# Seven block products in place of eight for a feed-forward product, accumulated and read in PSUM

## The chip, the cores and the metric

The kernel runs on one core of a Trainium2 chip. The metric is the device time of one launch in microseconds, as the median of several runs: 3187.57 us for the kernel before (3 runs, 3185.76 to 3188.36). The profile is of one execution with a span of 3186.1 us from the first to the last instruction.

## The reference

64 graphs of 256 nodes with 256 features each go through two layers. All data are f32, the adjacency is int32.

```
# layer 0
h = gat(x, adj, W1, a1); h = gat(h, adj, W2, a2)          # graph attention
h = layernorm(x + h)
ff = relu(h @ w_ff1 + b_ff1) @ w_ff2 + b_ff2              # (256 -> 1024 -> 256)
x = layernorm(h + ff)
# layer 1
q, k = x @ Wq + bq, x @ Wk + bk                           # 8 heads of 32
attn = softmax(q @ k.T / sqrt(32))
out = sum over r of (attn * (adj == r)) @ (x @ Wv[r] + bv[r])
x = layernorm(x + out @ Wo + bo)
ff = gelu(x @ W1 + b1) @ W2 + b2                          # (256 -> 1024 -> 256)
return layernorm(x + ff)
```

The product that is changed is `h @ w_ff1` of layer 0. Transposed, and for two graphs together, it is a matrix of 1024 x 256 weights by one of 256 x 512 activations.

## The kernel before, in words

The 64 graphs are worked on as 32 pairs. Each pair goes one way (`whole_way`): graph layers (`gat_layers`), feed-forward of layer 0, attention, feed-forward of layer 1, and a store. A matmul takes a stationary operand of 128 x 128 and a moving one of up to 512 columns, and writes into one of eight PSUM banks of 128 x 512 f32 (`bank`).

The order of the work is written by a planner in the kernel's own Python (`run`). Each pair's way is a generator. At each `yield` it names the events that the next step of TensorE needs, a stage that only one pair may be in ("gat", "ff", "attention"), and the number of banks that it takes. Work for the other engines is handed over with `put(engine, us, emit, *events, rank, ...)`: a piece with an estimated duration, which is emitted when its events have happened by the planner's clock; a lower rank goes first. `took(us)` moves TensorE's clock on. Up to three pairs are under way at a time. A TensorE step counts as sure when its inputs were ready `SLACK` microseconds ago by the planner's clock; among the sure ones those that are not in the stage "ff" go first; if none is sure, the one that is ready earliest is taken. What comes out is one fixed order of instructions for each engine; the waits between engines are added by the framework by what each instruction reads and writes.

Both feed-forwards are in `feed_forward`. For each of eight blocks `m` of 128 hidden features two products of 512 columns are accumulated over the two halves of the 256 input features (L538), and ScalarE adds the bias and applies relu or gelu on the way to SBUF (L541). The second product (L553) takes those eight tiles as stationary operands, 32 products of 256 columns. VectorE adds the result to the rows (L442 in `add_rows`), `layernorm` follows on VectorE (L454 to L464) with a power on GpSimd (L467), and `transposed` turns the rows by way of VectorE (L484) and DMAs to and from HBM on the queue of SyncE (`home`, `yT`).

The transposed activations `yT` lie so that a view `p k (b a) i` gives 512 columns of one input half `c`; k is one of two column halves of 256 columns, in runs of 32.

Other parts that the change touches: `load` brings in `xT`, the int32 adjacency `adjT` (three buffers) and `x` on SyncE's queue. `gat_layers` looks for nodes without neighbours in `adjT` (L387, L388), `gat_weights` uses it in L367, and `attention` multiplies the exponentials by it (L617). `attention` has tiles `qT`, `kT`, `oT`; scores read qT (L606), `products` write oT (L648), `into_rows` multiplies oT by Wo (L657). `relieve` (L732) takes a correction out of the biases at the start.

Of the kernel before, what the change touches and what calls it, by code (L numbers as in the profile page):

```python
# [27 lines left out]
SLACK = 1.5  # L28
# [4 lines left out]
def two_layers(ctx: ExitStack, tc: tile.TileContext, t: dict, out: bass.AP, flag: bass.AP):  # L33
# [91 lines left out]
    def bank():  # L125
# [13 lines left out]
                                             ("xT", 1), ("rows", 1), ("e", 2), ("adjT", 3), ("x", 4))}  # L139
# [137 lines left out]
    def load(pair, at=None):  # L277
# [7 lines left out]
        def adjT():  # L285
            to["adjT"] = io.tile([P, 4, N], I32, name="adjT", bufs=3)
            nc.sync.dma_start(to["adjT"], t["adjT"][rows].rearrange("b (c p) n -> p (b c) n", p=P))
# [7 lines left out]
        for emit in (xT, adjT, x):  # L295
            takes(emit.__name__, free[emit.__name__] != [])
            emit()
# [57 lines left out]
    def gat_weights(y, at, at_home, ratio, there, to, empty, b):  # L355
# [3 lines left out]
        def weigh(j):  # L359
# [7 lines left out]
            nc.vector.scalar_tensor_tensor(e[:, j], to["adjT"][:, k], empty[:, k:k + 1], e[:, j],  # L367
# [13 lines left out]
    def gat_layers(pair, to, loads):  # L381
# [3 lines left out]

        def largest():
# [7 lines left out]
        emptied = put("vector", 1.35, largest, loads[1], rank=2)  # L394
# [44 lines left out]
    def add_rows(y, p, b, *events):  # L439

        rows = y[:, of_graph(b), :].rearrange("p k d -> p (k d)")
        return put("vector", 0.6, lambda: nc.vector.tensor_tensor(rows, p, rows, ALU.add), *events, frees=["bank"])  # L442

    def layernorm(r, gb, b, *events):
# [4 lines left out]
        def statistics():  # L449
# [6 lines left out]
            nc.vector.tensor_scalar(rstd, mv[:, :, 1], EPS, None, ALU.add)  # L456
# [9 lines left out]
        there = put("vector", 1.15, statistics, *events)  # L466
        power = put("gpsimd", 0.8, lambda: nc.gpsimd.tensor_tensor(rstd, rstd, mhalf[:, :2], ALU.pow), there)  # L467
        return put("vector", 0.8, scale, power, put("vector", 0.8, centre, there))
# [55 lines left out]
    def feed_forward(y, normal, w, func, relieved, gb, pair, stage):  # L524
        w1, b1, w2 = w
        onwards = stage == 0
        if hurried(pair, stage):
            yield from transposed_on_tensor(y, normal)
        f, evacuated = [], []
        for m in range(NF):  # L530
            if m == 0:
                yield [normal[0], normal[1]], "ff", 1
                yT = [normal["yT"].rearrange("p b a (c k i) -> p c k (b a) i", c=KC, k=2)[:, c] for c in range(KC)]
            else:
                yield [], None, 1
            p1 = bank()
            for c in range(KC):
                nc.tensor.matmul(p1, lhsT=w1[:, c, m * P:(m + 1) * P], rhs=yT[c],  # L538
                                 start=c == 0, stop=c == KC - 1)
            f.append(work.tile([P, 512], F32, name="ff", bufs=NF))  # L540
            there = put("scalar", 0.6, lambda m=m, p1=p1: nc.scalar.activation(f[m], p1, func, bias=b1[:, m:m + 1]),  # L541
                        took(1.72), relieved, function="gelu" if func == AF.Gelu else None, frees=["bank"])
            evacuated.append(there)
        frees_at(clock["tensor"], ["yT"])
        for b in range(2):
            for j in range(2):
                k, split = 2 * b + j, NF // 2 if b or j else NF - 2
                for part in (range(split), range(split, NF)):
                    yield evacuated[part[0]:part[-1] + 1] if k == 0 else [], None, j == 0 and part[0] == 0
                    if j == 0 and part[0] == 0:  # L550
                        p2 = bank()
                    for m in part:
                        nc.tensor.matmul(p2[:, j * D:(j + 1) * D], lhsT=f[m][:, (2 * j + b) * P:(2 * j + b + 1) * P],  # L553
                                         rhs=w2[:, m, :], start=m == 0, stop=m == NF - 1)
                    there = took(0.43 * len(part))
# [3 lines left out]
        done_with("ff")  # L559

# [649 lines left out]
```

## Time and profile before

| what | value |
|---|---|
| median of the timed runs | 3187.57 us |
| span of the profiled execution | 3186.1 us |
| granted TensorE clock | 0.996 |
| HBM traffic | 137.51 MB read, 64.73 MB written |
| DMA engines' mean rate | 64 GB/s |

In the profile, PE is TensorE's matmuls, PEld its weight loads, DVE is VectorE, ACT is ScalarE, POOL is GpSimd, SP is SyncE; a "q" after it is the engine's sequencer. L538 is line 538 of the kernel. A group of instructions is written as: line, engine, operation, written tile <- read tiles, elements written <- read, count | busy us, mean ns of one | idle us of the engine just before them, and what ended that idle time. The chain of waits is the work that ended last, followed back from the end to the start. In a window of time the columns after its length are the busy us of PE, PEld, DVE, ACT and POOL with counts of instructions, then the granted clock, the share of the DMA engines and GB/s.

An f32 matmul is written as two instructions in the profile, so 16 products appear as x32.

### The profile page before, as it was taken

The page shows a single profiled execution, that of the slowest core. Times are in us where ns is not written, and L with a number is a line of the kernel's source. Part 1 is how long each engine was busy: PE and PEld are TensorE (multiplying, and loading weights), DVE is VectorE, ACT ScalarE, POOL GpSimd, SP SyncE. Part 2 cuts the span into 40 slices and gives each one's busy share as a digit, 9 for nine tenths or more (in the row PEclk, how much of TensorE's full clock was granted, in tenths as well). Part 3 has the DMA queues.
Part 4 walks back from the last instruction along what each step waited for, and adds up shares of the span by engine and source line. Part 5 has one row for each costly group of instructions (what it writes and reads, how often), then busy time and mean ns, then how long its engine had stood idle before and what let it go on. Part 6 is the DMA issues. An engine that isn't in the chain of part 4 may idle for free.

```text
span 3186.1 us, 45043 instructions
## 1 busy us (share of the span) xinstructions
PE 3150.4 (99%) x16830; PEld 2019.1 (63%) x16830; DVE 2210.0 (69%) x5525; ACT 1142.7 (36%) x2074; POOL 200.9 (6%) x262
## 2 busy tenths in 40 slices
PE   7999999999999999999999999999999999999998
PEld 6656756675576567566655765675666557656655
DVE  4677667767776776677677757766776777577564
ACT  3334333432432333334324323333342244333332
POOL 0000000000000000000000000000000000000000
PEclk8999999999999999999999999999999999999999
DMA  5112311321131123113211311231122113112200
GB/s 180 41 41 74 93 47 47 93 80 40 54 100 60 34 74 97 47 44 93 83 37 54 100 60 34 74 99 49 39 93 85 35 54 103 57 37 64 66 1 15
DMA packets 209857, 205.27 MB, mean 64 GB/s; under 512 B 22112, under 2 KB 169696, under 8 KB 209632
## 3 DMA queue, kind: packets, MB, share of 16 engines
q1 hardware_dynamic: 209632, 202.32, 20.4%
q8 instruction: 135, 2.21, 0.3%
q14 instruction: 90, 0.74, 0.1%
HBM read 137.51 MB, written 64.73 MB: 63 GB/s over the span
## 4 chain that ended last, share of the span: by engine, by line
PE 98%; DVE 1%; DMA 0%; ACT 0%; SPq 0%; issue 0%; POOL 0%; POOLq 0%; DVEq 0%
PE ps L538 28%; PE ps L553 28%; PE ps L574 7%; PE ps L566 7%; PE ps L635 7%; PE ps L606 4%; PE ps L416 4%; PE ps L429 4%; PE ps L657 3%; PE ps L400 3%; PE ps L638 2%; PE ps L732 0%; PE ps L515 0%; DMA w_L_gnn_w_ff1p<-in_L_gnn_w_ff1p 0%; DVE s L647 0%; DMA right<-in_L_gnn_W 0%
## 5 line engine op out<-in xcount | busy, mean ns | idle before, releaser
L617 DVE TENSOR_TENSOR m<-a,adjT 128x512 f32<-128x512 f32 x512 | 350.6, 685 | 208.1 <-ACT a L613 208.1
L553 PE MATMUL ps<-w_L_gnn_w_ff,ff 128*128 128x256 f32 x2048 | 463.3, 380 | 0.0
L553 PE MATMUL ps<-w_L_gnn_W,ff 128*128 128x256 f32 x2048 | 458.3, 380 | 0.0
L538 PE MATMUL ps<-yT,w_L_gnn_W1p 128*128 128x512 f32 x1024 | 456.9, 598 | 0.7 <-ACT yT L519 0.7
L538 PE MATMUL ps<-yT,w_L_gnn_w_ff1p 128*128 128x512 f32 x1024 | 452.2, 594 | 1.1 <-ACT yT L519 1.1
L553 PEld LDWEIGHTS ps<-w_L_gnn_w_ff,ff 128*128 128x128 f32 x2048 | 387.2, 190 | 90.9 <-issue 43.0
L553 PEld LDWEIGHTS ps<-w_L_gnn_W,ff 128*128 128x128 f32 x2048 | 388.2, 190 | 82.0 <-issue 30.4
L613 ACT ACTIVATE a<-ps 128x512 f32<-128x512 f32 x512 | 264.4, 602 | 392.7 <-issue 212.6
L467 POOL TENSOR_TENSOR rstd<-rstd,mhalf 128x2 f32<-128x2 f32 x256 | 200.2, 782 | 2978.8 <-DVE rstd L456 2978.8
L538 PEld LDWEIGHTS ps<-yT,w_L_gnn_W1p 128*128 128x128 f32 x1024 | 192.7, 191 | 224.9 <-issue 204.6
L538 PEld LDWEIGHTS ps<-yT,w_L_gnn_w_ff1p 128*128 128x128 f32 x1024 | 192.7, 190 | 224.7 <-issue 208.0
L647 DVE RECIPROCAL s<-ps 128x256 f32<-128x256 f32 x128 | 224.9, 1757 | 129.8 <-PE ps L638 129.8
L442 DVE TENSOR_TENSOR x<-ps,x 128x512 f32<-128x512 f32 x256 | 174.4, 681 | 200.8 <-PE ps L553 178.4
L541 ACT ACTIVATE ff<-ps,c_L_gnn_b_ff 128x512 f32<-128x512 f32 x256 | 175.8, 688 | 348.3 <-PE ps L538 348.3
L566 PE MATMUL ps<-wv,yTa 128*128 128x512 f32 x512 | 238.7, 599 | 0.0
L365 DVE SCALAR_TENSOR_TENSOR e<-rows,ratio 128x256 f32<-128x256 f32 x256 | 122.0, 477 | 149.7 <-DMA rows<-row 137.8
L375 ACT ACTIVATE xw<-xw,rs 128x258 f32<-128x258 f32 (+1 forms) x256 | 115.2, 501 | 288.3 <-DVE rs L370 288.3
L541 ACT ACTIVATE ff<-ps,c_L_gnn_b 128x512 f32<-128x512 f32 x256 | 169.1, 686 | 133.8 <-PE ps L538 133.1
L621 DVE TENSOR_TENSOR h<-a 128x256 f32<-128x256 f32 x512 | 213.5, 417 | 0.0
L454 DVE BATCH_NORM_STATS2 st<-x 128x6 f32<-128x256 f32 x512 | 208.2, 407 | 4.1
L391 ACT ACTIVATE xw<-ps 128x260 f32<-128x260 f32 (+1 forms) x256 | 97.7, 389 | 220.9 <-PE ps L416 111.4
L566 PEld LDWEIGHTS ps<-wv,yTa 128*128 128x128 f32 x512 | 94.6, 190 | 120.3 <-issue 117.9
(99 smaller groups left out, 3529.2 us busy)
## 6 DMA issues: line engine op xcount, KB each, us to landing
home<-yb SPq DMA_DIRECT2D x182, 256.0 KB, 2.0
yT<-home SPq DMA_DIRECT2D x728, 64.0 KB, 2.0
rows<-row SPq DMA_DIRECT2D x60, 512.0 KB, 4.1
xT<-in_xT SPq DMA_DIRECT2D x32, 512.0 KB, 3.6
adjT<-in_adjT SPq DMA_DIRECT2D x32, 512.0 KB, 4.0
x<-in_x SPq DMA_DIRECT2D x32, 512.0 KB, 4.0
out<-x SPq DMA_DIRECT2D x32, 512.0 KB, 3.4
w_L_gnn_w_ff1p<-in_L_gnn_w_ff1p SPq DMA_DIRECT2D x1, 1024.0 KB, 7.5
```

What stands on the lines that cost most here:

```text
L454: nc.vector.bn_stats(st[:, j, :], rows[j])
L467: power = put("gpsimd", 0.8, lambda: nc.gpsimd.tensor_tensor(rstd, rstd, mhalf[:, :2], ALU.pow), there)
L538: nc.tensor.matmul(p1, lhsT=w1[:, c, m * P:(m + 1) * P], rhs=yT[c], start=c == 0, stop=c == KC - 1)
L541: there = put("scalar", 0.6, lambda m=m, p1=p1: nc.scalar.activation(f[m], p1, func, bias=b1[:, m:m + 1]), took(1.72), relieved, function= ...
L553: nc.tensor.matmul(p2[:, j * D:(j + 1) * D], lhsT=f[m][:, (2 * j + b) * P:(2 * j + b + 1) * P], rhs=w2[:, m, :], start=m == 0, stop=m == N ...
L566: nc.tensor.matmul(ps, lhsT=yT[:, b, c, jc * P:(jc + 1) * P], rhs=wv[:, c].rearrange("p r m -> p (r m)"), start=c == 0, stop=c == KC - 1)
L574: nc.tensor.matmul(ps, lhsT=w[:, d, c * P:(c + 1) * P], rhs=yT[:, :, d, :], start=d == 0, stop=d == KC - 1)
L613: nc.scalar.activation(a[n][o], ps[o], AF.Exp)
L617: nc.vector.tensor_tensor(m[n][o], a[n][o], adj, ALU.mult)
L621: nc.vector.tensor_tensor(h[n][o], a[n][o][:, :N], a[n][o][:, N:], ALU.add)
L635: nc.tensor.matmul(po[o * DH:(o + 1) * DH, :N], lhsT=v[b][:, jc, at:at + DH], rhs=e[o][:, jc * N:(jc + 1) * N], start=r == jc == 0, stop=r ...
L647: there = put("vector", 1.68, lambda: nc.vector.reciprocal(s, po[:, N:]), there, rank=0)
```

## The change

The 1024 x 256 by 256 x 512 product is cut into 2 x 2 blocks on each side: A's four blocks of 512 x 128, B's four of 128 x 256. It is computed with seven products of blocks in place of eight, by a scheme in which the sums of blocks are made ahead and the partial results are shared between output blocks. The sums of weights are made once at the start (`block_sums`), the three more sums of activations for each pair on VectorE (`first_sum`, `other_sums`). For each of four block rows `t` of 128:

- `begin`: product 0 into half x of a bank, product 1 into half w of another, product 2 into half z of the first. ScalarE copies x out (u1), and VectorE adds w to it, which gives the first output block.
- `sixth`: product 3 on top of what stands in x; ScalarE copies the sum out (u2).
- `seventh`: product 4 on top of that; copied out (u3), and VectorE adds z to it, the fourth output block.
- `fourth`: product 6 on top of that; ScalarE takes relu of x, the third output block.
- `third`: product 5 on top of z; VectorE adds z to u2, the second output block.

Relu of the other blocks is taken from SBUF. The steps of four block rows are staggered, and the second feed-forward product is started in pieces among them. Layer 1's feed-forward keeps the old form (`whole`).

Besides: SLACK is 0.5 in place of 1.5, and some estimated durations differ. The adjacency is copied to bytes by ScalarE (`small_adj`, three buffers), and the int32 one keeps one buffer (pair 1 borrows a tile of `v`). oT takes qT's place. The addition of epsilon in the layernorm moves from VectorE to GpSimd. The first layer's weights come in four transfers. The buffers of the last check (`kept`) are borrowed from others.

```diff
-SLACK = 1.5
+SLACK = 0.5
...
-            nc.vector.tensor_scalar(rstd, mv[:, :, 1], EPS, None, ALU.add)
+        def root():
+            nc.gpsimd.tensor_scalar(rstd, mv[:, :, 1], EPS, None, ALU.add)
+            nc.gpsimd.tensor_tensor(rstd, rstd, mhalf[:, :2], ALU.pow)
...
+        def small_adj():
+            to["adj"] = io.tile([P, 4, N], U8, name="adj", bufs=3)
+            nc.scalar.activation(to["adj"], to["adjT"], AF.Copy)
...
+        def product(to, n, t, rhs, first=False):
+            nc.tensor.matmul(to, lhsT=w1[:, n, t * P:(t + 1) * P], rhs=rhs, start=first, stop=True, skip_group_check=True)
+            return took(0.43)
...
+        def begin(t):
+            q = of[t]
+            yield [normal[0], normal[1], summed[0], relieved] if t == 0 else [], "ff" if t == 0 else None, 2 if t % 2 == 0 else 1
...
+            xz = bank()
+            q["x"], q["z"] = xz[:, :N], xz[:, N:]
+            q["w"] = of[t - 1]["w"] if t % 2 else bank()
+            q["u1"] = evacuate(f[t][:, :N], q["x"], product(q["x"], 0, t, B[0][0], True))
+            there = product(q["w"][:, t % 2 * N:t % 2 * N + N], 1, t, B[1][0], t % 2 == 0)
+            q["c11"] = accumulate(f[t][:, :N], q["w"][:, t % 2 * N:t % 2 * N + N], q["u1"], there, frees=["bank"] * (t % 2))
+            product(q["z"], 2, t, sums[:, 0])
+
+        def sixth(t):
+            q = of[t]
+            yield [q["u1"], summed[1]], None, 0
+            q["u2"] = evacuate(f[t][:, N:], q["x"], product(q["x"], 3, t, sums[:, 1]))
+
+        def seventh(t):
+            q = of[t]
+            yield [q["u2"], summed[2]], None, 0
+            q["u3"] = evacuate(f[t + half][:, N:], q["x"], product(q["x"], 4, t, B[0][1]))
+            q["c22"] = accumulate(f[t + half][:, N:], q["z"], q["u3"])
+
+        def fourth(t):
+            q = of[t]
+            yield [q["u3"], summed[3]], None, 0
+            q["c21"] = activate(f[t + half][:, :N], q["x"], t + half, 0.36, product(q["x"], 6, t, sums[:, 2]))
+
+        def third(t):
+            q = of[t]
+            yield [q["c22"]], None, 0
+            c12 = accumulate(f[t][:, N:], q["z"], q["u2"], product(q["z"], 5, t, B[1][1]))
+            put("vector", 0.0, lambda: None, c12, q["c21"], rank=-1, lag=0.0, frees=["bank"])
+            evacuated[t + half] = activate(f[t + half][:, N:], f[t + half][:, N:], t + half, 0.36, q["c22"], q["c21"])
+            evacuated[t] = activate(f[t], f[t], t, 0.6, q["c11"], c12)
...
+        def first_by_blocks():
+            for t in range(half):
+                yield from begin(t)
+                if t > 1:
+                    yield from fourth(t - 2)
+                    yield from third(t - 2)
+                if t:
+                    yield from seventh(t - 1)
+                yield from sixth(t)
+            for step in (lambda: second(0, 0, (0, half), 1), lambda: second(0, 1, (0, half)),
+                         lambda: fourth(half - 2), lambda: third(half - 2), lambda: seventh(half - 1),
+                         lambda: second(0, 0, (1, half + 1)), lambda: second(0, 1, (1, half + 1)),
+                         lambda: fourth(half - 1), lambda: third(half - 1)):
+                yield from step()
...
-        qT, kT, oT = (work.tile([P, KC, 512], F32, name=n) for n in ("qT", "kT", "oT"))
+        qT, kT = (work.tile([P, KC, 512], F32, name=n) for n in ("qT", "kT"))
+        oT = qT
...
+    def block_sums(w, there):
+        for to, a, b, op in ((4, 0, 2, ALU.subtract), (2, 2, 6, ALU.add), (3, 2, 0, ALU.subtract), (5, 1, 3, ALU.subtract)):
+            there = put("vector", 0.65, lambda to=to, a=a, b=b, op=op: nc.vector.tensor_tensor(w[:, to], w[:, a], w[:, b], op),
+                        there, rank=0)
+        return there
```

## The prediction

> **What bounds the kernel now.** I read the busy shares first, then the chain of waits, then the groups of instructions, then the busy time in chosen windows.
>
> ```profile
> PE 3150.4 (99%) x16830; PEld 2019.1 (63%) x16830; DVE 2210.0 (69%) x5525; ACT 1142.7 (36%) x2074; POOL 200.9 (6%) x262
> PE 98%; DVE 1%; DMA 0%; ACT 0%; SPq 0%; issue 0%; POOL 0%; POOLq 0%; DVEq 0%
> ```
>
> The second line is the chain: 98% of the span is TensorE itself, so nothing but TensorE sets the time, apart from start and tail (in the first 70 us PE is busy 51.9, in the last 87 us 71.8). So TensorE time taken out is gained, if no new wait replaces it. The price of a product is best read in the chain in order of time (start, duration, instructions), because durations of single matmuls are modelled while runs of them are not:
>
> ```profile
> 674.12 12.09 PE ps L553 x56
> ...
> 691.38 13.73 PE ps L538 x32
> ```
>
> Each f32 product counts as two instructions. 13.73 us are the 16 products of 512 columns of one first feed-forward product: 0.858 each. 12.09 us are 28 products of 256 columns: 0.432 each. The groups:
>
> ```profile
> L553 PE MATMUL ps<-w_L_gnn_w_ff,ff 128*128 128x256 f32 x2048 | 463.3, 380 | 0.0
> L538 PE MATMUL ps<-yT,w_L_gnn_w_ff1p 128*128 128x512 f32 x1024 | 452.2, 594 | 1.1 <-ACT yT L519 1.1
> L541 ACT ACTIVATE ff<-ps,c_L_gnn_b_ff 128x512 f32<-128x512 f32 x256 | 175.8, 688 | 348.3 <-PE ps L538 348.3
> L391 ACT ACTIVATE xw<-ps 128x260 f32<-128x260 f32 (+1 forms) x256 | 97.7, 389 | 220.9 <-PE ps L416 111.4 <-PE ps L400 109.4
> L648 DVE TENSOR_TENSOR oT<-ps,s 128x256 f32<-128x256 f32 x128 | 53.8, 420 | 2.2
> L621 DVE TENSOR_TENSOR h<-a 128x256 f32<-128x256 f32 x512 | 213.5, 417 | 0.0
> L456 DVE TENSOR_SCALAR rstd<-mv 128x2 f32<-128x2 f32 x256 | 43.2, 169 | 8.9
> ```
>
> L538 has waited 1.1 us in the whole run: every one of its products was ready to go. The other lines are prices for what the change adds. Last, windows (duration, then busy us of PE, PEld, DVE, ACT, POOL):
>
> ```profile
> 1822.14:1834.16 12.02, 12.02 (x30) 5.32 (x29) 11.26 (x35) 5.61 (x10) 1.48 (x2) 1.00 0.50 153
> 1856.62:1870.35 13.73, 13.73 (x33) 6.08 (x32) 9.48 (x26) 5.34 (x8) 1.52 (x3) 1.00 0.36 111
> 1565.27:1856.62 291.35, 291.35 (x1538) 186.32 (x1536) 207.21 (x517) 106.14 (x192) 18.75 (x25) 1.00 0.21 66
> ```
>
> The third is one period of three pairs: 97.1 us a pair, PE never idle. The first two are this product of two of the three pairs. It runs there nearly alone on PE, and DVE is already 94% and 69% busy with layernorms and graph weights of other pairs. The third pair's (1605 to 1630) lies in pieces between attention steps.
>
> **What the Trainium skill says.** "PSUM — Partial Sum Buffer", section "The four PSUM rules": a first matmul clears the accumulate bits of the whole bank, later ones overwrite where the bit is clear and add where it is set, and a synchronised read in the midst of a group is allowed; so the seven-product scheme can work as written. The same page, "PSUM bank collisions raise a hardware error": two engines must not touch one bank in the same quadrant at once, even in different columns. No run here shows it; in the kernel before, PE fills a bank and one engine then empties it. "TensorE: Matmul & The Clock Gate", "Back-to-back issue gap": time goes with columns plus about 2.5 ns a matmul; the trace agrees (215.9 ns against half of 429.1, so 1.4 ns per instruction). "ScalarE: Activation LUTs", "What ACT_TABLE_LOAD costs": 186 ns plus 0.833 ns per column, 93 more for a bias pointer, that is 403 for 260 columns; the trace has 389.
>
> **The change part by part.**
>
> PE, per pair: 16 x 0.858 = 13.73 goes, 28 x 0.432 = 12.09 comes (the line shown). Saved 1.64, over 32 pairs 52.5 us. Twelve more weight loads of 0.190 lie under matmul instructions of 0.216, as they do at L553. The second product is only cut differently.
>
> ACT, per pair: 8 x 0.688 goes; 12 copies, 4 relus from PSUM and 4 from SBUF of 256 columns at 0.389 and 4 relus of 512 at 0.688 come: 10.5 - 5.5 = 5.0. The adjacency's copy to bytes has 1024 columns: by 0.389 for 260 and 0.688 for 512, some 1.0 to 1.3. In all +6 a pair, 194 us: 42% busy.
>
> DVE, per pair: 12 accumulations at 0.420 and 4 block sums at 0.417 come, 6.7; eight L456 go, 1.35. Net 5.4, 171 us: 75% busy. On average both have room. The byte adjacency I cost at nothing for L617 and L367: the int32 operand at L367 takes 485 ns, the f32 one at L365 477. It can hardly be slower than 5% of 685.
>
> POOL gets the epsilon add ahead of each power, about one more 0.78 us operation; L464 waited for POOL only 23.4 us in all. DVE time is not the end here: nothing, at most 2 us in the tail.
>
> SP: the weights come in four transfers in place of one (three more issues of about 0.43 us, same bytes); needed at 21 us for the bias, and the first product starts at 68. The block sums of the weights (4 x 0.68) also end long before that. The int32 adjacency has one buffer: a load placed early would hold SP, and the yT gathers queued behind it. It is freed by L387, early in a pair, so nothing; up to 5 us if not. oT in qT's place makes the next pair's L575 wait for L657, which ended at 1640.72 just as the next Wq product (1.72 us) began; that activation can't come before its end. Nothing.
>
> **Waits that come in.** Now the same PSUM half is filled, read by ACT, and filled on top, four times per block row; PE depends on ACT and DVE inside the product. The round trip: ACT starts 0.20 after the last instruction's slot ends (the product from 1822.14 gives its four slots at 1823.86, L541 starts at 1824.06), the copy takes 0.39, and PE goes on 0.05 after an ACT end (yT done at 3147.35, L538 at 3147.40): 0.64. `begin` issues three products in one step, first into x, third into z of the same bank. The first copy is emitted after them, so, with banks kept apart, it starts only when the third is through: 0.86 later than the planner thinks. Then for block row 0 `sixth` follows at once: PE stands 0.64. For row 1 one product lies between: 0.64 - 0.43 = 0.21. From row 2 three lie between (1.30): none. At the end the second product of rows 3 and 7 has four products (1.73) ahead of it, against relu of half a tile, accumulate, relu of 512: 0.20 + 0.39 + 0.42 + 0.20 + 0.69 + 0.05 = 1.95, and one more slip between ACT and DVE in that bank: about 0.3. Sum 1.15 a pair if nothing is put between. Below, such a wait can be zero (other pairs' steps fill it, or the bank isn't shared in practice); above, see the third rival. I take it as met in two of three pairs, since one of three lies among attention steps: 0.77 x 32 = 24.5 us.
>
> SLACK 0.5 lets the planner pick a step whose inputs were ready 0.5 us ago where it wanted 1.5. PE has nothing to win from that in the steady part, and loses if ACT or DVE run late; I take it with the waits.
>
> **Sum.** 3186.1 - 52.5 + 24.5 + 1 (tail) = 3159.1 against this execution's span; the timed runs' median lies 1.5 us above it (3187.57), so 3161.
>
> **Rivals.** A change of under 0.2%, 6.4 us, can't be told from none.
>
> 1. All of it is gained: the waits find other work. For: ACT is at 36%, and the steps are staggered by four products or more. Against: two of three such products run alone. 3187.6 - 52.5 = 3135.
> 2. The gain is eaten to the last: waits of 1.6 a pair. About 3187, within 0.2%.
> 3. The other side: DVE paces the product. 6.7 us of its work come into windows where it already has 9.5 to 11.3 of 12 to 13.7. Its pieces are not interrupted (statistics and its kin are about 1.2 us: 1822.01 to 1823.20), so an accumulation stands up to 1.2 us in line, and PE's `fourth` and `third` stand behind it, as both use that bank. From copy to end of the accumulation 0.64 + 0.20 + 0.42 = 1.26 must fit in the four products (1.73) before `fourth`: 0.47 is left. The gain is gone when this costs (1.64 - 0.77) / 4 = 0.22 per block row; at 0.4 per row it is 1.6 + 0.77 - 1.64 = 0.73 a pair, +23 us: 3211. Against it: the planner gives accumulations first rank and knows the lengths.
>
> **How the numbers follow.** Forecast 0.48, full gain 0.18, nothing 0.10, slower 0.24. Faster is 0.48 + 0.18 = 0.66. For the range: the full gain with a little more from start or tail is 3133; the third rival's price is 3212. Both signs lie inside; the forecast's own range is 3140 (a quarter of the waits) to 3180 (waits of 1.4 a pair).
>
> **What would show it.** PE busy some 52 us less, with 256-column products at 216 ns a slot. Idle time of PE before the product's lines, put down to ACT, about 25 us; put down to DVE and over 30 us, the third rival. ACT near 42%, DVE near 75%. A gap ahead of the fourth product of a block row in a lone window, 0.6 us, would show the shared bank; its lack, the first rival. Wrong altogether if the attention or graph lines begin to wait: then it is the planner's order, not the product.

## The result, and the profile after

The changed kernel takes 3196.16 us (median of 6 runs, 3193.16 to 3197.79) against 3186.95 us for the kernel before (6 runs): a ratio of 1.0028, 95% interval 1.0015 to 1.0041. By the bound of the prediction, 0.2%, it is slower, though the interval's lower end lies inside that bound. The forecast of 3161 is 35 us too low. The profiled executions differ by 9.5 us (3195.6 against 3186.1), as the medians do, so the two traces can be set beside each other.

From the page of the changed kernel, the busy shares, and the chain of waits by engine:

```profile
PE 3131.6 (98%) x17598; PEld 2151.9 (67%) x17598; DVE 2336.6 (73%) x5785; ACT 1309.7 (41%) x2612; POOL 267.5 (8%) x518
PE 86%; DVE 4%; DMA 4%; ACT 3%; issue 1%; SPq 1%; POOL 0%; ACTq 0%; DVEq 0%; POOLq 0%
```

PE is busy 18.8 us less than before (3150.4), and the span is longer all the same. The chain says what kind of time came in: it was 98% PE, and is 86% now, with VectorE, ScalarE and, new, DMA.

The groups of the changed product, its copy and its accumulation (line, engine, operation, tiles and count | busy us, mean ns | idle before, releaser):

```profile
L571 PE MATMUL ps<-yT,w_L_gnn_w_ff1p 128*128 128x256 f32 x1024 | 269.6, 380 | 0.0
L571 PE MATMUL ps<-sums_yT,w_L_gnn_w_ff1p 128*128 128x256 f32 x768 | 231.4, 393 | 18.8 <-ACT ff L575 15.3 <-DVE ff L578 0.2
L575 ACT ACTIVATE ff<-ps 128x256 f32<-128x256 f32 x384 | 142.8, 382 | 235.2 <-PE ps L571 231.2
L578 DVE TENSOR_TENSOR ff<-ps,ff 128x256 f32<-128x256 f32 x384 | 160.7, 419 | 135.1 <-ACT ff L581 55.3 <-ACT ff L575 54.2 <-PE ps L571 24.2
```

The products that wait are those with block sums as moving operand: `sixth` and `fourth` are among them. (Busy time of matmuls overlaps, so these 501 us are no measure of the product.) The waits of TensorE and of its weight loads (engine, line, what was waited for: us, times, longest):

```profile
PEld ps L571 <- ACT ff L575: 37.2, 52, 0.9
PEld ps L571 <- DVE ff L578: 23.3, 61, 0.7
PEld ps L424 <- ACT xw L379: 19.3, 16, 3.0
PE ps L571 <- ACT ff L575: 15.3, 31, 0.5
PE ps L424 <- ACT xw L379: 13.2, 10, 2.6
```

Two places: the changed product (L571), and a product of the graph layers (L424, L416 before), which the change doesn't touch and whose weight loads before waited 0.7 us for the same. A weight load's wait and its matmul's wait overlap, and the first begins early, so neither column is the time lost. For that I took, from the trace, the starts of TensorE's matmul instructions. The time from one start to the next is a slot. The median slot of a line is its normal price, and what lies above it is a loss: a gap where it is 0.11 us or more, a restart where it is about 0.10 (see the last section). Us over the whole span:

| | before | after | difference |
|---|---|---|---|
| normal slots of layer 0's first product | 439.3 | 387.1 | -52.2 |
| normal slots of all else | 2666.6 | 2661.8 | -4.8 |
| gaps ahead of L571 | 0 | 31.7 | +31.7 |
| gaps ahead of layer 0's second product, L627 | 0 | 5.0 | +5.0 |
| gaps ahead of L424 | 0 | 13.8 | +13.8 |
| other gaps (first 70 us: 16.2 and 16.6) | 21.6 | 22.9 | +1.3 |
| restarts, 425 and 561 | 42.1 | 56.2 | +14.1 |
| small deviations | -0.4 | -0.2 | +0.2 |
| first to last start | 3169.1 | 3178.3 | +9.2 |

(439.3 is half of what L538 had in both layers. The products on parts of the array, the attention's and the one that turns rows at the start and the end, L515 before and L526 after, are counted with all that passes in their slots. Of the 4.8 us in the second line 3.7 come from L515, which waits at the end of the kernel before.) So the gain is there to within a microsecond, and 66 us of losses came against it: about 51 in and around the product, about 14 in the graph layers.

Shortly before its end the changed kernel is further behind than these 9.2 us. The last matmul of the last pair's graph layers starts at 2987.2 us before and at 3004.5 after, 17.3 us later. What follows up to the last start takes 190.0 us before and 181.5 after. About 3 of these 8.5 us can be the new product's saving; for the rest see SLACK below.

The timeline of the changed kernel where a product starts (start, us, what; in brackets idle time before and its releaser), and the window over it (length, then busy us of PE, PEld, DVE, ACT, POOL, clock, DMA share, GB/s):

```profile
1574.25 1.03 PE L571 MATMUL ps<-yT,w_L_gnn_w_ff1p 128*128 128x256 f32 x4
1575.11 0.59 PE L571 MATMUL ps<-sums_yT,w_L_gnn_w_ff1p 128*128 128x256 f32 x2
1575.74 0.38 ACT L575 ACTIVATE ff<-ps 128x256 f32<-128x256 f32 x1 [3.98 <-PE ps L571]
1576.18 0.70 PE L571 MATMUL ps<-sums_yT,w_L_gnn_w_ff1p 128*128 128x256 f32 x2 [0.47 <-ACT ff L575]
```
```profile
1574.25:1587.07 12.82, 12.30 (x56) 10.01 (x54) 9.90 (x30) 7.10 (x18) 2.77 (x6) 1.00 0.13 41
```

The first line is the products into x and w of `begin`, the second the one into z. They come at 0.432 a product: x is done at about 1574.68. Its copy starts at 1575.74, which is 0.20 after z is done. `sixth` starts at 1576.18, where the slot after z would have ended at 1575.54: 0.64 us of standing, and its second instruction comes 0.10 late. In the window DVE is busy 77% and ACT 55%; neither is full.

### The profile page after: what moved, and what is told of

The parts are those of the page before. It is cut to its first block, busy times and chain, and to the rows that moved or that the text cites. A ratio compares the mean times of both kernels' runs of the same rounds, so it can differ in the third digit from the quotient of the medians.

```text
span 3195.6 us, 47479 instructions
## 1 busy us (share of the span) xinstructions
PE 3131.6 (98%) x17598; PEld 2151.9 (67%) x17598; DVE 2336.6 (73%) x5785; ACT 1309.7 (41%) x2612; POOL 267.5 (8%) x518
## 4 chain that ended last, share of the span: by engine, by line
PE 86%; DVE 4%; DMA 4%; ACT 3%; issue 1%; SPq 1%; POOL 0%; ACTq 0%; DVEq 0%; POOLq 0%
PE ps L627 24%; PE ps L571 11%; PE ps L636 10%; PE ps L688 7%; PE ps L680 7%; PE ps L750 7%; PE ps L721 4%; PE ps L424 4%; PE ps L437 4%; PE ps L772 4%; PE ps L408 3%; DMA rows<-row 2%; PE ps L753 2%; ACT ff L581 1%; DVE m L732 1%
## 5 line engine op out<-in xcount | busy, mean ns | idle before, releaser
L627 PE MATMUL ps<-w_L_gnn_w_ff,ff 128*128 128x256 f32 x2048 | 473.1, 382 | 1.3
L627 PE MATMUL ps<-w_L_gnn_W,ff 128*128 128x256 f32 x2048 | 459.6, 381 | 0.0
L732 DVE TENSOR_TENSOR m<-a,adj 128x512 f32<-128x512 f32 x512 | 351.2, 686 | 127.7 <-ACT a L728 127.7
L627 PEld LDWEIGHTS ps<-w_L_gnn_W,ff 128*128 128x128 f32 x2048 | 386.5, 190 | 75.7 <-issue 26.1
L627 PEld LDWEIGHTS ps<-w_L_gnn_w_ff,ff 128*128 128x128 f32 x2048 | 384.4, 190 | 72.1 <-ACT ff L581 10.5
L466 POOL TENSOR_SCALAR rstd<-mv 128x2 f32<-128x2 f32 x256 | 71.8, 280 | 2899.9 <-DVE mv L463 2701.6
L571 PE MATMUL ps<-yT,w_L_gnn_w_ff1p 128*128 128x256 f32 x1024 | 269.6, 380 | 0.0
L578 DVE TENSOR_TENSOR ff<-ps,ff 128x256 f32<-128x256 f32 x384 | 160.7, 419 | 135.1 <-ACT ff L581 55.3
L571 PE MATMUL ps<-sums_yT,w_L_gnn_w_ff1p 128*128 128x256 f32 x768 | 231.4, 393 | 18.8 <-ACT ff L575 15.3
L575 ACT ACTIVATE ff<-ps 128x256 f32<-128x256 f32 x384 | 142.8, 382 | 235.2 <-PE ps L571 231.2
L571 PEld LDWEIGHTS ps<-yT,w_L_gnn_w_ff1p 128*128 128x128 f32 x1024 | 193.6, 190 | 33.0 <-issue 4.2
```

Source lines behind the costliest of these rows:

```text
L571: nc.tensor.matmul(to, lhsT=w1[:, n, t * P:(t + 1) * P], rhs=rhs, start=first, stop=True, skip_group_check=True)
L732: nc.vector.tensor_tensor(m[n][o], a[n][o], adj, ALU.mult)
```

## The experiments

The theory: (a) the shared bank makes the copy late, as the prediction had it, and (b) the losses ahead of L424 come from another edit. The rivals: VectorE has too much to do; or the order of the steps is to blame, above all SLACK. Ratios are to the kernel before in runs on the same chip, with the 95% interval. "Gaps" and "restarts" are those of the table above, each from one trace.

### All but the product

`rest` has every other edit, and the old eight products (and with them the first layer's weights in one transfer again).

```diff
-        half, by_blocks = NF // 2, stage == 0
+        half, by_blocks = NF // 2, False
```

> Layer 0's first product in the old form (16 products of 512 columns), all other edits of the change kept: SLACK 0.5, byte adjacency, epsilon on GpSimd, oT in qT's place, estimated durations. If the seven products alone bring the waits: as before, within 5 us (3187). If SLACK 0.5 or the other edits cost something by themselves, as the 12.6 us of waits ahead of L424 in the changed kernel suggest: slower than before by 10 to 20 us (3197 to 3207), with gaps ahead of the graph layer's products.

3189.34 us, 1.0008 (1.0001 to 1.0015). So the product by itself, on top of the other edits, costs 3196.2 - 3189.3 = 7 us where it should save. And the other edits have a loss of their own: gaps of 14.8 us ahead of L424, as large as in the changed kernel. They don't come from the seven products. Neither branch of what was expected is met whole: the time is nearly that of the first, the gaps are those of the second.

### x in a bank of its own

```diff
-            xz = bank()
-            q["x"], q["z"] = xz[:, :N], xz[:, N:]
-            q["w"] = of[t - 1]["w"] if t % 2 else bank()
+            wz = bank()
+            q["x"], q["w"], q["z"] = bank()[:, :N], wz[:, :N], wz[:, N:]
...
```

Every `begin` takes two banks, eight for the four rows in place of six, and they are given free one by one.

> The changed kernel with x alone in a bank, and w and z of one block row together in another (8 banks for four rows in place of 6). Theory bank: the first copy waited for the third product only because both are of one bank, so the wait ahead of sixth falls from 0.64 to under 0.1 for row 0 (20 us over 32 pairs, with the restarts 24) and from 0.14 to none for row 1 (4 to 6 us), and fourth no longer waits for VectorE's reading of z (9 to 14 us): some 30 to 40 us faster than the changed kernel, about 3160. Theory round trip: TensorE to ScalarE to TensorE is too slow at any placing, or ScalarE is busy: the gaps stay, 3190 to 3200. Two more banks may bring waits for banks: then new gaps at begin.

3166.49 us, 0.9940 (0.9926 to 0.9953): 30 us less than the changed kernel. The start of the product, in its timeline:

```profile
1554.27 1.03 PE L571 MATMUL ps<-yT,w_L_gnn_w_ff1p 128*128 128x256 f32 x4
1554.90 0.38 ACT L575 ACTIVATE ff<-ps 128x256 f32<-128x256 f32 x1 [2.32 <-PE ps L571]
1555.13 1.03 PE L571 MATMUL ps<-sums_yT,w_L_gnn_w_ff1p 128*128 128x256 f32 x4
```

The copy now starts 0.63 us after the product began, where it was 1.49: 0.86 earlier, two products, to the digit. It ends at 1555.28, and `sixth`, which is in the last line's four instructions, follows z without a break. What L571's instructions waited for (idle us, times), in the changed kernel:

```profile
  ACT ff L575: 52.4, 83
  DVE ff L578: 23.6, 62
```

and with x alone:

```profile
  ACT ff L575: 2.6, 6
  DVE ff L578: 2.1, 3
```

Both are gone, VectorE's too, with the same number of VectorE instructions. Gaps ahead of L571 fall from 31.7 to 2.1 and all restarts from 56.2 to 39.8. That is 46 us; the runs gained 30. What took the difference can be seen: the slots of the attention's products on parts of the array grew by 19 us, the scores from 138.0 to 150.6 (L719) and the products with v from 222.5 to 227.0 (L748), with the output sums 2 more. The growth is in single pairs: the scores of five of the 32 have slots of 6.6 to 7.0 us in place of 4.3. In one of these stretches they stand in line behind VectorE:

```profile
1081.44 1.21 PE L719 MATMUL ps<-qT,kT 32*128 32x256 f32 x4 [0.29 <-DVE s L757]
1082.84 1.85 PE L719 MATMUL ps<-qT,kT 32*128 32x256 f32 x12 [0.20 <-DVE s L757]
```

### SLACK

Three runs: SLACK 1.5 in the changed kernel (`slack15`) and with x alone (`x_alone_s15`), and 0.5 in the kernel before (`b_slack05`), each with that one line changed:

```diff
-SLACK = 0.5
+SLACK = 1.5
```

> The changed kernel with SLACK 1.5 again, nothing else. Theory order: the 12.6 us ahead of L424 (graph layer steps taken before their weights are there) come from SLACK 0.5, so they go: 10 to 15 us faster than the changed kernel, about 3183; the gaps ahead of sixth stay at 0.64 a pair. Theory product: SLACK has no part in it, the time stays within 4 us of 3196.

> Both: x alone in its bank and SLACK 1.5. If the two causes add: 40 to 50 us faster than the changed kernel, 3146 to 3156, faster than before by over 1%. If SLACK is not a cause: as x alone with SLACK 0.5.

> The kernel before with SLACK 0.5, nothing else. The changed kernel without its seven products waits 11.6 us ahead of L424 (L416 here). If SLACK makes that wait: gaps of 8 to 15 us ahead of L416 appear here too, and the time is 0 to 12 us over before (the tail's 7.6 us of gaps may go). If the byte copy of the adjacency, GpSimd's epsilon or the estimated durations make it: no such gaps, within 4 us of before.

`slack15`: 3214.04, 1.0082 (1.0068 to 1.0096), 18 us above the changed kernel. `x_alone_s15`: 3175.24, 0.9958 (0.9945 to 0.9972), 9 above x alone. `b_slack05`: 3181.44, 0.9981 (0.9975 to 0.9988), some 5 below before. In all three 0.5 is the better value: the theory that SLACK 0.5 spoils the order falls, and what I had expected of the first two was of the wrong sign. The gaps ahead of L416 in `b_slack05` are 3.9 us, so SLACK isn't what makes most of the 14.8 in `rest`.

Where 0.5 gains is another matter. Between 70 and 3000 us PE has no gap in the kernel before, and 5.1 us of gaps in `b_slack05`, which is 6.9 us later at the last matmul of the last pair's graph layers (2994.1 against 2987.2). It wins at the end alone: from there to the last start the same instructions take 177.4 us in place of 190.0. In the kernel before, a product that turns the last pairs' rows waits there for the layernorm, and in `b_slack05` it doesn't:

```profile
PE ps L515 <- DVE x L464: 6.7, 2, 4.9
```

With 1.5 this wait is there in the other two kernels as well (L526, 5.0 us in each). Of the 15 us between the last starts of `slack15` and the changed kernel, 9.0 are there by the last graph matmul, and 6.3 come behind it. In `slack15` the gaps ahead of L424 are gone, and yet it is slower. The gaps in the product grow (35.4 ahead of L571, 9.9 ahead of the second product), and the attention's slots with them (222.5 to 236.4, 138.0 to 145.2, 62.5 to 66.9: 26 us). This wait, which the changed kernel's list has in no such size, goes with it:

```profile
PEld ps L750 <- DVE m L732: 15.4, 24, 0.8
```

The attention's product stands for the masked exponentials of VectorE. The order of the steps matters by 10 to 20 us, then, but this edit of it was a gain, at the end of the kernel as much as within it.

### The planner told of the later copy

`truth` leaves the banks as they are, and tells the planner that the first copy hangs on the third product.

```diff
-            q["u1"] = evacuate(f[t][:, :N], q["x"], product(q["x"], 0, t, B[0][0], True))
+            product(q["x"], 0, t, B[0][0], True)
             there = product(q["w"]...)
-            product(q["z"], 2, t, sums[:, 0])
+            q["u1"] = evacuate(f[t][:, :N], q["x"], product(q["z"], 2, t, sums[:, 0]))
```

> The changed kernel with its banks, but the first copy (u1) hangs on the third product's end by the planner's clock, as it does on the chip. If the wait ahead of sixth is the shared bank, telling the planner moves it little where no other pair's step is ready: row 0 keeps some 0.6 us in most pairs, the sum of gaps in the product falls from 45 to 25 to 40 us, 3185 to 3196 in all. If the planner's ignorance was the harm: the gaps are filled with other work and the time falls below 3175, as with x alone.

3180.83, 0.9982 (0.9976 to 0.9989): 15 us less than the changed kernel, between the two forecasts. The planner can now put another pair's steps ahead of row 0's `sixth`, which waits in 13 of 32 pairs in place of 31. Gaps ahead of L571 fall to 25.0 and restarts to 52.2. So half of what x alone gains can be had without a further bank: the plan was made from a wrong time, and that is a part of the harm. (Some 11 of the 17 us between the two traces are in these gaps and in restarts; the rest comes with the other order, in places that the edit doesn't name.)

### The load of VectorE

`rest_dve` is `rest` with 16 additions of 256 columns more per pair on VectorE, of the first product's output halves into a tile that nothing reads. Its results are not used; the output is that of `rest`. `x_alone_pool` is x alone, with the four block sums of activations for each pair (three in tiles of their own, one in place) on GpSimd.

```diff
+            if stage == 0:
+                for n in range(2):
+                    put("vector", 0.42, lambda n=n: extra(m, n), evacuated[m], rank=-1)
```
```diff
-            nc.vector.tensor_tensor(in_blocks[0], B[0][1], B[0][0], ALU.subtract)
+            nc.gpsimd.tensor_tensor(in_blocks[0], B[0][1], B[0][0], ALU.subtract)
...
-            nc.vector.tensor_tensor(to, a, b, ALU.subtract)
+            nc.gpsimd.tensor_tensor(to, a, b, ALU.subtract)
```

> The old product with all other edits, and 16 additions of 256 columns on VectorE at first rank for each pair, in layer 0's first product; their results are not used. It is the VectorE work of the seven products (6.7 us a pair) without their waits. x alone has only 6.5 us of gaps in the product, yet gains 23 of 46 us against the old product; 19 us more stand within the attention products (L719, L748, L751). If VectorE's load makes these: 8 to 20 us over the run without the additions (3189), with gaps in the attention products. If banks make them: within 4 us of 3189.

> x alone in its bank, and the four block sums of activations on GpSimd in place of VectorE (1.7 of 6.7 us a pair). If VectorE's load paces attention: 4 to 12 us faster than x alone (3155 to 3162). If it doesn't: the same within 4 us (3166), or slower where GpSimd's sums come late (gaps ahead of begin's third product and sixth).

`rest_dve`: 3193.49, 1.0021 (1.0013 to 1.0029), 4 us above `rest`, for 16 x 0.42 x 32 = 215 us of VectorE work. The 8 to 20 us that this load was expected to cost did not come, and the slots of the attention's products are those of `rest` to the tenth (137.7, 222.5 and 62.5). `x_alone_pool`: 3155.17, 0.9899 (0.9884 to 0.9914), 11 below x alone, for four sums of some 0.42 us, 54 us of VectorE work. The scores' slots went back from 150.6 to 143.2, the products' with v from 227.0 to 224.3, 10 us together; two pairs have long scores in place of five. So VectorE's load by itself does not make the loss in the attention, and in another order a quarter of it taken away makes it smaller. The edit moves the planner's order too, and no run parts the two. There is no general price per microsecond of VectorE work here.

### The adjacency

`rest_adj2` is `rest` with two int32 buffers in place of one; `rest_i32` has the adjacency as before, int32 throughout with three buffers, and no byte copy.

```diff
...
-            else:
-                to["adjT"] = io.tile([P, 4, N], I32, name="adjT")
+            to["adjT"] = io.tile([P, 4, N], I32, name="adjT", bufs=2)
...
```
```diff
...
+            to["adjT"] = to["adj"] = io.tile([P, 4, N], I32, name="adjT", bufs=3)
...
-            nc.scalar.activation(to["adj"], to["adjT"], AF.Copy)
...
```

> As the kernel without the seven products (3189.3), with bytes, but two buffers for the int32 adjacency in place of one, so that its load no longer hangs on L395 of the pair ahead. If the time of the load is the cause: 3178 to 3185. If the copy to bytes on ScalarE (1.05 us ahead of L395) is: 3187 to 3191.

> The old product, SLACK 0.5, and the other edits except the adjacency's: int32 with three buffers again, no copy to bytes. The kernel before with SLACK 0.5 alone has 3181.4 us and 4 us of gaps ahead of the graph layer's product (L416); with the other edits (without the seven products) it is 3189.3, with 13 us of such gaps. In the trace of one, the int32 load, which its one buffer lets go only after L395, runs beside the store of `home`, and the gather of yT behind which rows is queued waits for it. If the single buffer is the cause: 3178 to 3184, the gaps under 6 us. If GpSimd's epsilon, the durations or oT are: 3187 to 3191, the gaps stay.

3178.70, 0.9974 (0.9964 to 0.9984), and 3178.92, 0.9973 (0.9963 to 0.9984). Both are as expected if the single buffer is the cause. The two agree: the byte copy costs nothing, and the single int32 buffer costs 10.5 us. The gaps ahead of that graph product are 2.1 and 2.3 in their traces, and 14.8 in `rest`, 13.0 of it in nine pairs, every third one. One of these places in the timeline of `rest`, SyncE's queue first:

```profile
914.74 0.38 SPq L500 DMA_DIRECT2D home<-yb  x1
915.23 0.40 SPq L291 DMA_DIRECT2D adjT<-in_adjT  x1
915.67 0.64 SPq L348 DMA_DIRECT2D row<-blocks  x1
917.77 1.74 SPq L506 DMA_DIRECT2D yT<-home  x4
920.61 0.34 SPq L352 DMA_DIRECT2D rows<-row  x1
925.74 0.48 DVE L369 SCALAR_TENSOR_TENSOR e<-rows,ratio 128x256 f32<-128x256 f32 x1 [10.12 <-DMA rows<-row]
929.40 2.88 PE L424 MATMUL ps<-xw,e 128*128 128x258 f32 x12 [0.80 <-ACT xw L379]
```

and the same place in `rest_adj2`:

```profile
912.17 0.38 SPq L496 DMA_DIRECT2D home<-yb  x1
912.65 0.55 SPq L344 DMA_DIRECT2D row<-blocks  x1
915.26 1.73 SPq L502 DMA_DIRECT2D yT<-home  x4
917.08 0.38 SPq L348 DMA_DIRECT2D rows<-row  x1
921.78 0.48 DVE L365 SCALAR_TENSOR_TENSOR e<-rows,ratio 128x256 f32<-128x256 f32 x1 [8.72 <-DMA rows<-row]
925.88 3.64 PE L420 MATMUL ps<-xw,e 128*128 128x258 f32 x16
```

The single buffer is free again once the copy and the search for neighbours of the pair before are through, and so the next pair's 512 KB load falls into that pair's first graph layer, right ahead of a write of 4 KB, `row`. `rows` (`rows<-row`) reads back what that write has put down, and VectorE, and PE after it, wait for `rows`. The store to `home`, and the gather of its data that is issued when it has landed, are little of it: the gather comes 3.0 us after the store in `rest` and 3.1 in `rest_adj2`. It is `row`. Here it lands 4.9 us after its issue with the load and 2.8 without, and in `rest` `rows` is issued as soon as it has landed. VectorE starts 11.0 us after the store's issue in place of 9.6. (`rows` themselves take 5.0 us in `rest` and 4.3 in `rest_adj2`, in the median of the nine: in `rest` a store of `out` has come to stand ahead of them.) Medians of the nine pairs (us from issue to landing):

| | `home` | `row` | from the issue of `row` to the landing of `rows` |
|---|---|---|---|
| rest | 3.08 | 4.80 | 9.98 |
| rest_adj2 | 3.18 | 2.86 | 9.04 |
| after | 3.65 | 4.60 | 10.31 |
| adjlate (below) | 3.00 | 2.72 | 8.71 |

To see it in the changed kernel, `adjlate` keeps the single buffer, and lets the load wait until the first graph layer of the pair before is through with its rows:

```diff
-put("sync", 0.45, emit, rank=3, ...) for emit in (xT, adjT, x)
+put("sync", 0.45, emit, *([spread_out[pair - 1]] if emit is adjT else []), rank=3, ...) for emit in (xT, adjT, x)
...
+        put("vector", 0.0, lambda: None, *there, rank=-1, lag=0.0, event=spread_out[pair])
```

> The changed kernel; only the load of the next pair's int32 adjacency waits, by the planner, until the first graph layer's rows have landed, so that it can't run beside the store of home and the small transfer of row. If the 10.5 us that the single buffer cost without the seven products are in the changed kernel too: 3184 to 3190 (changed: 3196), and the 12.6 us of gaps ahead of L424 fall under 5. If they were an effect of that other kernel's order alone: 3193 to 3200.

3173.73, 0.9962 (0.9948 to 0.9975): 22 us below the changed kernel, more than expected. The load is now behind `rows` on the queue, `row` lands early (last line of the table), and the gaps ahead of the graph product fall from 13.8 to 0.5 us. Of the 23.4 us between the two traces' last starts, 13.3 are gaps at this line, 4.8 gaps ahead of the changed product, 3.9 restarts. That the product also gains I had not expected. Through which steps it gains is open.

### The planner's rate for transfers

In `xap_rate`, on `x_alone_pool`, the planner reckons with 200 in place of 380 KB per us, so that it sees transfers land later.

```diff
-                    moved[0] = max(moved[0], clock[engine]) + piece["kb"] / 380.0
+                    moved[0] = max(moved[0], clock[engine]) + piece["kb"] / 200.0
```

> x alone in its bank and block sums on GpSimd (3155.2), and the planner reckons with 200 in place of 380 KB per us for transfers, since the 512 KB loads take 3.8 to 4.9 us and those of 256 KB beside them up to 5.5. If transfers that the planner thinks too short make what is left of the gaps ahead of L424 and L437 (12 us): 3 to 12 us faster. If its order only gets worse for it: 3155 to 3170.

3169.49, 0.9945 (0.9931 to 0.9959): 14 us above `x_alone_pool`, a miss. The gaps ahead of L424 went, as was wanted (8.6 to 0). But the attention's slots grew by 26 us (scores 143.2 to 158.6, products with v 224.3 to 231.4, output sums 63.3 to 66.5), and gaps of 6.6 came ahead of layer 1's second product. Delaying all transfers in the plan is too coarse; delaying the one load is not.

### Both together

`xap_adjlate` is `x_alone_pool` with the late load.

> The same late load with x alone in its bank and the block sums on GpSimd (3155.2; gaps of 12 us ahead of L424 and L437). If the causes add: 3143 to 3150, 1.2 to 1.4% faster than before. If the load's place is no cause there: 3153 to 3158.

3144.39 us, 0.9873 (0.9858 to 0.9888): 42 us faster than the kernel before, the best here, and as expected if the causes add.

All runs, medians in us (gaps and restarts of one trace each; L424 and L571 stand for the same products in every kernel, and their columns leave out the first 70 us):

| kernel | us | ratio | gaps | of these at L571 | at L424 | restarts |
|---|---|---|---|---|---|---|
| before | 3186.95 | 1 | 21.6 | - | 0 | 42.1 |
| after | 3196.16 | 1.0028 | 73.4 | 31.7 | 13.8 | 56.2 |
| rest | 3189.34 | 1.0008 | 31.4 | - | 14.8 | 41.5 |
| rest_adj2 | 3178.70 | 0.9974 | 17.9 | - | 2.1 | 41.1 |
| rest_i32 | 3178.92 | 0.9973 | 19.3 | - | 2.3 | 43.0 |
| rest_dve | 3193.49 | 1.0021 | 30.9 | - | 13.4 | 40.3 |
| b_slack05 | 3181.44 | 0.9981 | 22.4 | - | 3.9 | 42.7 |
| slack15 | 3214.04 | 1.0082 | 65.9 | 35.4 | 0 | 49.9 |
| truth | 3180.83 | 0.9982 | 61.0 | 25.0 | 14.5 | 52.2 |
| adjlate | 3173.73 | 0.9962 | 53.2 | 27.0 | 0.5 | 52.3 |
| x_alone | 3166.49 | 0.9940 | 40.0 | 2.1 | 7.7 | 39.8 |
| x_alone_s15 | 3175.24 | 0.9958 | 30.8 | 0.2 | 0.4 | 36.3 |
| x_alone_pool | 3155.17 | 0.9899 | 35.3 | 1.9 | 8.6 | 41.0 |
| xap_rate | 3169.49 | 0.9945 | 31.4 | 0.4 | 0 | 37.2 |
| xap_adjlate | 3144.39 | 0.9873 | 30.3 | 6.9 | 0 | 41.9 |

A second int32 buffer along with `x_alone_pool` was not run.

## Why the prediction was wrong

**The saving** was right: 52.5 us forecast, 52.2 in the slots, at 0.432 a product as read from L553.

**The shared bank** was right in kind. It was the mechanism forecast, with the price forecast: the first copy starts two products late, `sixth` of row 0 stands 0.64 us (largest 0.70), and row 1's `sixth` lost 4.4 us in all, against 0.21 x 32 x 2/3 = 4.5 in the sum. The runs show it by x alone, where the copy is 0.86 us earlier and the waits vanish. Whether a rule of the chip demands the order or the framework's own dependencies for a bank wrote it in, no run tells; with the two kept apart by bank the question doesn't come up. The section "PSUM bank collisions raise a hardware error" in the Trainium skill's "PSUM — Partial Sum Buffer", named in the prediction, would forbid the copy beside the third product, and nothing here contradicts it.

**The size of the waits** was wrong, 24.5 forecast and 51 measured (31.7 + 5.0 in gaps and 14.1 in restarts). Three terms of it:

- "I take it as met in two of three pairs" failed. Row 0's wait came in 31 of 32 pairs, 20.3 us in place of 13.7. Pairs that lie among attention steps wait as well, because the planner believes that the copy is early and puts nothing between; `truth` shows it, with 13 of 32.
- At the end of a product, 0.3 a pair, hence 6.4, was forecast. The second product of rows 3 and 7 lost 5.0 and row 3's `fourth` 4.1; row 1's `fourth` lost 3.3 that the sum didn't have at all.
- No restart was reckoned with. They are 136 more than before, of about 0.10 us each; 123 of the changed kernel's stand right after a gap, and 4 of those before.

**SLACK**: "PE has nothing to win from that in the steady part, and loses if ACT or DVE run late" held for the kernel before, where `b_slack05` falls 6.9 us behind up to the last graph matmul. What the prediction left out is the end of the kernel: the 1 us that its sum adds for the tail had the wrong sign. Behind that matmul `b_slack05` is 12.6 us shorter than before, `rest` 11.3, the changed kernel 8.5. For the changed kernel the sentence failed in the steady part too: `slack15` is 9.0 us behind by that matmul. In sum 0.5 wins 5 us in the kernel before, 18 in the changed kernel, 9 with x alone. Without it the change would have been slower by 0.8%.

**SP** is the step whose failure decides the sign beside the waits: "It is freed by L387, early in a pair, so nothing; up to 5 us if not." The buffer is indeed freed early, and just that puts the next load into the middle of the first graph layer, right ahead of the write of `row`. I named the queue and the gathers behind it, but reckoned with an issue that is held up, not with a small transfer that lands late behind a large one. It costs 10.5 us in `rest`; taken out of the changed kernel, the time falls by 22.

The three measured terms give the sum anew: -52.2 + 51 + 13.8 = +12.6, less some 3.5 of other slots and gaps (most of it waits at the end that are gone), +9.2. What the prediction named as making it "wrong altogether" happened: a graph line, L424, began to wait. But the cause was the transfers' order on SP, not the choice of TensorE's steps, and it stood beside the product's waits, not in their place.

**Rival 3**, VectorE pacing the product, gave 3211, and the time lies nearer to it than to the forecast. Its mechanism isn't what happened. L571's idle time put down to VectorE, 23.6 us, falls to 2.1 with x alone at the same VectorE load; `fourth` lost 7 us in rows 1 and 3 together, not 0.4 in every row, which would be 51. Of the 11 us that came back with the block sums on GpSimd, 10 are in the attention's slots.

**Loads** were right: ACT 41% (42 forecast), DVE 73% (75), the byte adjacency nothing (`rest_adj2` and `rest_i32` are equal). The epsilon on GpSimd was not run alone; all other edits together with two int32 buffers (`rest_adj2`, 3178.7) are no slower than SLACK 0.5 alone (3181.4).

**A slip without weight**: the "1.4 ns per instruction" of the prediction is half of what its two figures give, 2 x 215.9 - 429.1 = 2.7 ns, so they agree better with the 2.5 cited there than was said.

What stays open: why the attention's slots grow by 10 to 30 us in some orders (x alone, both runs with SLACK 1.5, and `xap_rate`) and not in others. It comes in single pairs: in `slack15` the products of the masked exponentials with v have slots of 4.6 us in place of 3.5 in every third pair. The clock doesn't explain it there, since the granted clock of `slack15` is 1.00 from 70 to 3160 us. VectorE is what these products wait for in the lines shown, but `rest_dve` has its load without the growth.

## What to carry to other kernels

A partial result that is read between two accumulations wants a bank for itself: sharing its bank with a product that is emitted ahead of the read delays the read by that product (to 1.49 us after the start, from 0.63), and a planner that doesn't know it delays the next step too. When the sum of an edit is a difference of large terms, cost the number of waits and their restarts first; a saving of 1.6 us a pair bears only two waits. And freeing a buffer early is not free: look at what the refill will stand in front of on its queue, and tie the load to an event after the urgent small transfers. Last, ask of a gain where in the run it lies: SLACK 0.5 lost in the steady part of the kernel before and won more at its end.

## What was not expected of the hardware

- **A restart costs a tenth of a microsecond.** After a wait, the slot that follows is 320 ns in place of 217. In the timeline after, `sixth` starts at 1576.18 and its second instruction at 1576.50. It is the time of a second weight load that isn't made ahead, I believe: the load for the second instruction ends 0.02 us before it starts. The runs show the 0.10, in 561 slots against 425. A wait is not the only way to it: 123 of the 561 come right after a gap, and 198 right after products on parts of the array.
- **A gap of 2.7 us can slow what follows, and doesn't always.** In `rest`, and then in the changed kernel, PE stands for about the same time ahead of L424:

```profile
1223.67 2.79 PE L424 MATMUL ps<-xw,e 128*128 128x258 f32 x8 [2.65 <-ACT xw L379]
```
```profile
347.06 1.14 PE L424 MATMUL ps<-xw,e 128*128 128x258 f32 x4 [2.60 <-ACT xw L379]
```

From 1224.95 on the slots of `rest` are 430 ns in place of 217, and in the changed kernel they stay at 217. The windows (length, busy us, granted clock, DMA share, GB/s) of the two:

```profile
1223.67:1226.46 2.79, 2.79 (x9) 2.26 (x10) 0.47 (x3) 1.52 (x4) 0.00 (x0) 0.69 0.00 0
```
```profile
347.06:350.50 3.44, 3.44 (x16) 2.98 (x17) 0.48 (x3) 2.30 (x6) 0.00 (x0) 1.00 0.00 0
```

The granted clock is 0.69 in the first and 1.00 in the second. The Trainium skill, "TensorE: Matmul & The Clock Gate", section "Part 1: The HAM clock gate (the "warmup" mystery)", has the clock halve after an idle window of about 3.4 us; the halving agrees, but here a shorter idle time was enough for it once and not the other time. With x alone the same is seen after the stretch of scores shown above, which uses 32 of 128 rows and has breaks: the 512-column products behind it take 850 to 1015 ns an instruction in place of 430, at a clock of 0.66 (a window of x alone):

```profile
1084.50:1089.00 4.50, 4.50 (x8) 2.04 (x8) 4.50 (x10) 4.27 (x7) 0.00 (x0) 0.66 0.00 0
```

So a thin or broken stretch can be paid twice: of the gaps at L424 in `rest`, 1.5 us are such slow slots. The changed kernel has none there.

- **A small transfer lands late behind a large one.** The 4 KB of `row` land 1.7 us after their issue in the median of the 31 places of `rest` with no 512 KB transfer issued in the 6 us ahead of them. With the adjacency's 512 KB issued 0.4 to 0.9 us ahead of them they take 4.3 us (19 places) and 4.8 (nine); at the same places of `rest_adj2`, without that load, 2.1 and 2.9. The 256 KB store issued 0.5 us ahead of the load takes the same with it and without, 3.1 and 3.2. The load's own landing, 4.0 us in the median before and 4.8 after, is 6.0 in `adjlate`, at no harm.
- **A reader of bytes costs VectorE what one of int32 does**: 485 ns for 256 columns in both kernels (L367 before, L371 after).
